# Transposing softmax probabilities on TensorE as two 16-bit halves of each word

## The chip, the cores and the metric

The kernel runs on one core of a Trainium2 chip. A core has a matrix engine (TensorE, PE in the profile; its weight loads are listed apart as PEld), a vector engine (VectorE, DVE), a scalar engine (ScalarE, ACT), GpSimd (POOL) and a queue for transfers (SyncE, SP). TensorE reads SBUF and writes PSUM; a matmul holds one operand in the array (it is loaded by a weight load) and streams the other through it. The metric is the time of one execution on the device in microseconds.

## The reference

The reference is a gated cross-attention block followed by a gated, quantized feed-forward block, on `x` of shape (2, 2048, 512) and a context of 77 tokens for each of the 2 batches.

```python
q = (layernorm(x) @ Wq.T + bq)            # 16 heads of 32
k, v = ctx @ Wk.T + bk, ctx @ Wv.T + bv   # 77 keys
attn = softmax(q @ k.T / sqrt(32))        # per head, 2048 x 77
x = x + tanh(g_xattn) * ((attn @ v) @ Wo.T + bo)
h = gelu(qlinear(layernorm(x), w1, b1))   # 512 -> 2048, 8-bit grid, per-tensor scale
x = x + tanh(g_ffn) * qlinear(h, w2, b2)  # 2048 -> 512
```

Everything is float32. `qlinear` rounds its input and its weight to 255 levels by the largest magnitude of the whole tensor.

## The kernel before

The 4096 rows are worked in 8 blocks of 512 rows (`NB = 8`, `TB = 512`), each as 4 row tiles of 128 (`NT = 4`). The kernel has three stages: attention for all blocks (up to about 423 us of the profiled execution, with the end of the last block's output projection and the scale of the quantization up to about 449 us), the first feed-forward product with GELU, and the second product with the output.

The change lies in the attention stage. The 16 heads are worked as 4 groups of 4 heads (`NG = 4`, `HG = 4`), and a block has 8 steps `s`: a step is one head group and one half (2 of the 4 row tiles). The functions of a step, with their lines:

- `project_q` (L257): 4 accumulating fp32 matmuls (8 instructions) make `pq`; ScalarE adds the bias into `qT`.
- `softmax` (L270): TensorE makes the scores of 2 row tiles and 4 heads in PSUM (`ps`, L279, 8 instructions); VectorE takes the maximum (L288) and subtracts it (L292); ScalarE exponentiates in place (L298); VectorE sums (L300) and inverts (L302); GpSimd multiplies (L303). The result `e`, 128 rows by 2 x 4 x 77 float32 probabilities, lies in one of 3 SBUF buffers.
- `transpose_a` (L309), called twice for each step (`u` = 0 and 1): TensorE transposes the four 128 x 77 pieces of one row tile into one PSUM tile `pta` (L316), where the probabilities are the loaded operand (77 columns) and the identity the streamed one (128 columns), and ScalarE copies the PSUM tile into `aT` (L317), 77 keys by 4 heads by 512 rows.
- `apply_v` (L319): when a head group's `aT` is complete, 4 fp32 matmuls (8 instructions, `pc`) multiply by the values; ScalarE copies to `cT` (L333).
- `project_o` (L335): the output projection of one row tile of the block before (`po`, 8 instructions); VectorE adds it to `x`.
- `transpose_x` (L241): normalizes a row tile of the next block, transposes it in fp32 (`ptx`, L251, 128 columns loaded), and ScalarE copies to `xnT` (L252).

The PSUM pool `ps_t` has two buffers, shared by `pta` and `ptx`: a third transposed tile cannot be written before the first one has been copied out. `ps_s` (scores) and `ps_p` (projections and `pc`) have two each.

The loop goes over the blocks and their 8 steps. In each step it issues the softmax of two steps ahead, then the first `transpose_a`, then by the step's number an `apply_v` and a `project_o` (even steps), a `project_q` or two `transpose_x` (odd steps), and the second `transpose_a`. This program order is the priority with which a planner lists the instructions of each engine; it works with estimated costs, and may put later work ahead where an instruction is not ready by its estimate. Each engine then runs its list in order. Only the start of the kernel and the feed-forward stage have an order written out by hand. Around the step, `weight_step` puts the quantization of the feed-forward weights on VectorE, and `load_x` puts the loads of later blocks on SP's queue; a `project_q` of the next block needs all four of its `xnT` copies.

`ident` is a 128 x 128 float32 identity and `identb` the same in bf16 (L123); the latter is used before the change for the transposes of quantized rows alone (`px`, L180).

Of the kernel before, what the change touches and what calls it, by code (L numbers as in the profile page):

```python
# [7 lines left out]

F32 = mybir.dt.float32
BF16 = mybir.dt.bfloat16  # L10
AF = mybir.ActivationFunctionType
ALU = mybir.AluOpType
AX = mybir.AxisListType
# [2 lines left out]
P = 128  # L16
D = 512
KC = D // P
HEADS = 16
DK = D // HEADS  # L20
NK = 77
HG = P // DK
# [20 lines left out]
def tile_flamingo_gated_block(  # L43
# [20 lines left out]
    nc = tc.nc  # L64
# [56 lines left out]
    ident = const.tile([P, P], F32, name="ident")  # L121
    make_identity(nc, ident)
    identb = const.tile([P, P], BF16, name="identb")  # L123
    nc.vector.tensor_copy(identb, ident)
# [4 lines left out]

    w1q = const.tile([P, KC, FF], BF16, name="w1q")  # L130
    xqT0 = const.tile([P, KC, TB], BF16, name="xqT0")
    w2q = const.tile([P, FC, D], BF16, name="w2q")
    mean2 = const.tile([P, NB, NT, 2], F32, name="mean2")
# [16 lines left out]
    def scale_of(maxima, name, psum, tag):  # L150


        m = const.tile([P, 1], F32, name=f"m_{name}")
        nc.vector.tensor_reduce(m, maxima, AX.X, ALU.max)
        diag = small.tile([P, P], F32, tag="diag", name=f"diag_{name}", bufs=1)
        nc.vector.tensor_scalar(diag, ident, m, None, ALU.mult)
        pg = psum.tile([P, 512], F32, tag=tag, name=f"pg_{name}")
        nc.tensor.matmul(pg[:, :P], ones, diag, start=True, stop=True)
        g = const.tile([P, 1], F32, name=f"g_{name}")
        nc.vector.tensor_reduce(g, pg[:, :P], AX.X, ALU.max)  # L160
        s = const.tile([P, 1], F32, name=f"s_{name}")
        nc.vector.tensor_scalar(s, g, MIN_RANGE, 1.0 / QP, ALU.max, ALU.mult)
        inv = const.tile([P, 1], F32, name=f"inv_{name}")
        nc.vector.reciprocal(inv, s)
        return s, inv
# [12 lines left out]
    def transpose_q(dst, src):  # L178
        for kc in range(KC):
            nc.tensor.transpose(dst[:, kc, :], src[:, kc * P : (kc + 1) * P], identb)  # L180
# [10 lines left out]
    with actx:  # L191
        ps_s = actx.enter_context(tc.tile_pool(name="ps_s", bufs=2, space=PSUM))
        ps_t = actx.enter_context(tc.tile_pool(name="ps_t", bufs=2, space=PSUM))
# [5 lines left out]
        def project_k(b, g):  # L199
# [10 lines left out]
            for j in range(HG):  # L210
# [3 lines left out]
                if j % 2:  # L214
                    nc.scalar.activation(dst, pk[r, :NK], AF.Identity, bias=bias)
                else:
# [15 lines left out]
        ln, xnT, qT, aT, cT, es = {}, {}, {}, {}, {}, {}  # L232
# [24 lines left out]
        def project_q(i, g):  # L257
# [9 lines left out]
            qT[i, g] = work.tile([P, TB], F32, tag="qT", name=f"qT{i}_{g}", bufs=5)  # L267
            nc.scalar.activation(qT[i, g], pq, AF.Identity, bias=bq_sb[:, g : g + 1])

        def softmax(i, s):  # L270
# [26 lines left out]
            ).ins  # L297
            last["ACT"] = nc.scalar.activation(e, e, AF.Exp, scale=SCALE).ins  # L298
            sm = small.tile([P, 2, HG], F32, tag="sm", name=f"sm{n}")
# [9 lines left out]
        def transpose_a(i, s, u):  # L309
            g, half = divmod(s, 2)  # L310
            t = 2 * half + u
            if t == 0:
                aT[i, g] = work.tile([NK, HG, TB], F32, tag="aT", name=f"aT{i}_{g}", bufs=3)
            pt = ps_t.tile([P, KC, P], F32, tag="pt", name=f"pta{i}_{s}_{u}")
            for j in range(HG):
                nc.tensor.transpose(pt[:NK, j, :], es[i, s][:, u, j, :], ident)  # L316
            nc.scalar.copy(aT[i, g][:, :, t * P : (t + 1) * P], pt[:NK, :, :])  # L317

        def apply_v(i, g):  # L319
            pc = ps_p.tile([P, TB], F32, tag="pp", name=f"pc{i}_{g}")  # L320
# [116 lines left out]
        for i in range(NB):  # L437
            for s in range(2 * NG):
                if s + 2 < 2 * NG:
                    last = softmax(i, s + 2)  # L440
                elif i + 1 < NB:
                    last = softmax(i + 1, s + 2 - 2 * NG)
                transpose_a(i, s, 0)

                if i == 0 and s < 2:
# [3 lines left out]
                if i == 0 and s == 2:  # L449


                    with tc.issue_after(last["ACT"]):
                        nc.scalar.activation(tg, tg, AF.Tanh)
                    with tc.issue_after(last["POOL"]):
# [10 lines left out]
                if i + 1 < NB:  # L465
# [3 lines left out]
                    if s in (3, 5):  # L469
                        for t in (s - 3, s - 2):  # L470
                            transpose_x(i + 1, t)
                transpose_a(i, s, 1)
                if s in (5, 7) and i + 1 < NB:
                    project_q(i + 1, (s - 5) // 2)
# [15 lines left out]
                t = s - NT if i == 0 else s // 2  # L490
# [11 lines left out]
        warm = small.tile([P, 1], F32, tag="warm", name="warm")  # L502
        nc.scalar.activation(warm, cT[NB - 1, NG - 1][:, 0:1], AF.Gelu)
        for t in range(NT):
# [7 lines left out]
        s_x, inv_x = scale_of(xmax, "x", ps_p, "pp")  # L512
        xq0 = work.tile([P, NT, D], BF16, tag="xnT", name="xq0", bufs=1)
        for t in range(NT):
# [4 lines left out]
            else:  # L519
                nc.scalar.activation(v, v, AF.Copy, bias=MAGIC, scale=inv_x)  # L520
                last = nc.vector.tensor_scalar(vq, v, MAGIC, None, ALU.subtract).ins
        for t in range(NT):
            px = ps_t.tile([P, KC, P], BF16, tag="pt", name=f"px0_{t}")
            transpose_q(px, xq0[:, t, :])
# [21 lines left out]
    with ExitStack() as fctx:  # L546
# [22 lines left out]
        for i in range(NB):  # L569
# [4 lines left out]
            for a in range(GT):  # L574
                G = gtile(f"G{i}_{a}")
                for v in range(GF // 2):
# [18 lines left out]
                    k = (i * GT + a) * 2 + v  # L595
                    n = 1 if k == NB * GT * 2 - 1 else 2
# [129 lines left out]
```

## Time and profile before

| | |
|---|---|
| median of 3 runs | 692.16 us (690.68 to 694.86) |
| profiled execution | 692.1 us, span 690.0 us from the first to the last instruction |
| mean granted TensorE clock | 0.985 |
| TensorE busy | 651.0 us (94%) |
| VectorE busy | 518.4 us (75%) |
| ScalarE busy | 342.9 us (50%) |
| GpSimd busy | 200.7 us (29%) |
| transposes of the probabilities, L316 | 512, 280 ns from start to end each |
| copies out of PSUM, L317 | 128, 579 ns each |

A row of groups names the line, the engine, the operation, the tile written and the tiles read, the shapes and the count; behind the bar stand the busy time and the mean length of one, behind the second bar the idle time of the engine just before, with what ended it. In the timeline the first column is the start, the second the length of a run of like instructions, merged. In the table of stretches the columns are the length, the busy times with the number of instructions (in the order PE, PEld, DVE, ACT, POOL, where an engine has any), the granted clock, the share of the transfer engines, and GB/s. The chain that ended last lists what the end waited for, step by step; "issue" is time in which nothing seen in the profile was waited for.

### The profile page before, as it was taken

How to read it: one execution, taken by the hardware profiler on the slowest of the kernel's cores; microseconds unless marked ns; L12 is line 12 of the kernel's file. 1: busy time of each engine (PE TensorE's matmuls, PEld its weight loads, DVE VectorE, ACT ScalarE, POOL GpSimd, SP SyncE). 2: the span in 40 equal slices, each digit the busy share in tenths (PEclk: the TensorE clock that was granted, in tenths of full speed). 3: DMA queues.
4: the chain of work that ended last, by engine and by line, in shares of the span. 5: the costliest groups of instructions: out<-in, count | busy, mean ns of one | idle time of the engine just before them, and what ended most of it. 6: DMA issues, size and time to landing. Idle time of an engine off the chain costs nothing.

```text
span 690.0 us, 8178 instructions
## 1 busy us (share of the span) xinstructions
PE 651.0 (94%) x3027; PEld 324.3 (47%) x3048; DVE 518.4 (75%) x799; ACT 342.9 (50%) x472; POOL 200.7 (29%) x160
## 2 busy tenths in 40 slices
PE   4999999999999999999999999599999979999987
PEld 2655555455555455555455454244444424444433
DVE  3674686996996996975965757899998779865452
ACT  2455443344443344444344333179898979344540
POOL 2234323233233233233333332100000029991000
PEclk9999999999999999999999999799999989999999
DMA  9901100031131131100000000059999608798872
GB/s 299 353 2 58 65 1 0 1 119 65 62 123 61 62 117 66 62 0 1 1 0 1 1 16 1 0 153 353 318 312 358 183 9 345 262 347 321 315 275 76
DMA packets 41663, 89.09 MB, mean 129 GB/s; under 512 B 18763, under 2 KB 18763, under 8 KB 35480
## 3 DMA queue, kind: packets, MB, share of 16 engines
q1 hardware_dynamic: 39752, 87.21, 36.2%
q10 hardware_dynamic: 1872, 1.37, 0.7%
q8 instruction: 24, 0.39, 0.2%
q14 instruction: 15, 0.12, 0.1%
HBM read 51.34 MB, written 33.55 MB: 123 GB/s over the span
## 4 chain that ended last, share of the span: by engine, by line
PE 77%; DMA 8%; DVE 8%; ACT 4%; issue 2%; POOL 0%; SPq 0%; ACTq 0%; DVEq 0%
PE ph L581 16%; PE po L338 16%; PE pq L260 15%; PE pta L316 8%; DMA Gb<-h 7%; PE ps L279 6%; PE pf L643 6%; PE pc L325 6%; PE ptx L251 2%; ACT Gb L634 2%; DMA x<-in_x 1%; PE pvv L223 1%; PE pk L203 1%; DVE xf L169 1%; DVE tm L360 1%
## 5 line engine op out<-in xcount | busy, mean ns | idle before, releaser
L303 POOL TENSOR_TENSOR e<-e,rs 128x616 f32<-128x616 f32 x64 | 78.4, 1226 | 255.3 <-DVE rs L302 192.4
L643 PE MATMUL pf<-w2q,hq 128*128 128x512 bf16 x502 | 114.9, 388 | 8.4 <-DVE hq L635 4.6
L260 PE MATMUL pq<-xnT,wq_sb 128*128 128x512 f32 x256 | 117.9, 604 | 2.0 <-ACT xnT L252 2.0
L338 PE MATMUL po<-wo_sb,cT 128*128 128x512 f32 x256 | 117.6, 604 | 0.0
L581 PE MATMUL ph<-xqT,w1q 128*128 128x512 bf16 x501 | 111.3, 382 | 1.3 <-DVE xqT L526 0.5
L317 ACT COPY aT<-pta 77x512 f32<-77x512 f32 x128 | 72.4, 579 | 77.8 <-PE pta L316 77.7
L588 ACT ACTIVATE G<-ph,b1s,s 128x512 f32<-128x512 f32 x128 | 99.5, 777 | 14.0 <-PE ph L581 3.1
L657 POOL TENSOR_TENSOR x<-x,b_sb 128x512 f32<-128x512 f32 x32 | 57.8, 1848 | 125.2 <-DVE b_sb L614 125.2
L643 PEld LDWEIGHTS <-hq 128*128 128x128 bf16 x512 | 50.6, 100 | 72.4 <-issue 8.3
L598 DVE TENSOR_REDUCE hmax<-G 128x1 f32<-128x1024 f32 (+1 forms) x65 | 76.5, 1197 | 10.4 <-ACT G L588 10.3
L316 PE MATMUL pta<-ident,e 128*77 128x128 f32 x512 | 79.3, 280 | 1.7 <-ACT aT L317 1.2
L338 PEld LDWEIGHTS po<-wo_sb,cT 128*128 128x128 f32 x256 | 46.2, 189 | 71.7 <-issue 70.4
L581 PEld LDWEIGHTS <-w1q 128*128 128x128 bf16 x512 | 50.3, 99 | 62.0 <-issue 2.1
L316 PEld LDWEIGHTS pta<-ident,e 128*77 128x77 f32 x512 | 59.8, 147 | 40.6 <-issue 34.3
L298 ACT ACTIVATE e<-e 128x616 f32<-128x616 f32 x64 | 45.9, 717 | 60.2 <-DVE e L292 56.1
L288 DVE TENSOR_REDUCE mx<-ps 128x8 f32<-128x616 f32 x64 | 49.9, 780 | 30.3 <-PE ps L279 30.1
L260 PEld LDWEIGHTS pq<-xnT,wq_sb 128*128 128x128 f32 x256 | 46.8, 193 | 51.2 <-issue 47.2
L634 ACT ACTIVATE Gb<-Gb,inv_h 128x2048 f32<-128x2048 f32 x24 | 47.6, 1999 | 45.9 <-DMA Gb<-h 43.9
L300 DVE TENSOR_REDUCE sm<-e 128x8 f32<-128x616 f32 x64 | 50.4, 789 | 24.2 <-ACT e L298 23.9
L635 DVE TENSOR_SCALAR hq<-Gb 128x2048 bf16<-128x2048 f32 x24 | 38.2, 1600 | 30.5 <-ACT Gb L634 30.5
L292 DVE TENSOR_TENSOR e<-ps,mx 128x616 f32<-128x616 f32 x64 | 50.9, 796 | 2.9
L279 PE MATMUL ps<-kb,qT 64*128 64x154 f32 x512 | 52.7, 319 | 0.2
(89 smaller groups left out, 594.4 us busy)
## 6 DMA issues: line engine op xcount, KB each, us to landing
h<-G SPq DMA_DIRECT2D x24, 1024.0 KB, 6.2
Gb<-h SPq DMA_DIRECT2D x24, 1024.0 KB, 8.2
raw_w<-in_w2T SPq DMA_DIRECT2D x8, 1024.0 KB, 5.0
out_y<-x SPq DMA_DIRECT2D x32, 256.0 KB, 4.4
x<-in_x SPq DMA_DIRECT2D x7, 1024.0 KB, 5.4
raw_w<-in_w1T SPq DMA_DIRECT2D x4, 1024.0 KB, 11.7
x<-in_x SPq DMA_DIRECT2D x4, 256.0 KB, 3.5
wq_sb<-in_wqT ACTq DMA_DIRECT2D x1, 1024.0 KB, 9.6
```

The lines of the kernel that those rows point to most:

```text
L260: nc.tensor.matmul(pq, wq_sb[:, kc, g * P : (g + 1) * P], xnT[i][:, kc, :], start=(kc == 0), stop=(kc == KC - 1),)
L279: nc.tensor.matmul(ps[:, q, u * RK : (u + 1) * RK], qT[i, g][r, t * P : (t + 1) * P], kblk[i // NBB][r, g, :], start=True, stop=True,)
L303: last["POOL"] = nc.gpsimd.tensor_tensor(e4, e4, rs[:, :, :, None].to_broadcast([P, 2, HG, NK]), ALU.mult).ins
L316: nc.tensor.transpose(pt[:NK, j, :], es[i, s][:, u, j, :], ident)
L317: nc.scalar.copy(aT[i, g][:, :, t * P : (t + 1) * P], pt[:NK, :, :])
L338: nc.tensor.matmul(po, cT[i, g][:, t * P : (t + 1) * P], wo_sb[:, g, :], start=(g == 0), stop=(g == NG - 1),)
L581: nc.tensor.matmul(ph, w1q[:, kc, fc * P : (fc + 1) * P], cur[:, kc, :], start=(kc == 0), stop=(kc == KC - 1),)
L588: nc.scalar.activation(G[:, 2 * v + u, :], ph, AF.Gelu, bias=b1s[:, fc : fc + 1], scale=s1,)
L598: nc.vector.tensor_reduce(hmax[:, k + u : k + u + 1], G[:, 2 * v + u : 2 * v + u + n, :], AX.XY, ALU.max, apply_absolute_value=True,)
L634: nc.scalar.activation(rest, rest, AF.Copy, bias=MAGIC, scale=inv_h)
L643: nc.tensor.matmul(po[t], hq[:, fc, t * P : (t + 1) * P], w2q[:, fc, :], start=(fc == 0), stop=(fc == FC - 1),)
L657: nc.gpsimd.tensor_tensor(y, y, b2_sb, ALU.add)
```

## The change

A float32 word is seen as two 16-bit halves. For each head, TensorE transposes the low halves and the high halves apart, as bf16 with the bf16 identity, so that the PSUM tile has 4 heads x 2 halves x 128 rows of 16 bits: the same 2 KB a partition as before. A transpose moves the bits as they are. ScalarE's copy reads the PSUM tile as unsigned 16-bit integers in its order, and writes each half to its place in the words of `aT`, that is with a distance of two 16-bit elements. The number of copies stays, each with twice the elements; the number of transposes doubles. The loaded operand of a transpose is 77 elements of 2 bytes that lie 4 bytes apart.

```diff
+U16 = mybir.dt.uint16
...
-            pt = ps_t.tile([P, KC, P], F32, tag="pt", name=f"pta{i}_{s}_{u}")
+
+            pt = ps_t.tile([P, HG, 2, P], BF16, tag="pt", name=f"pta{i}_{s}_{u}")
             for j in range(HG):
-                nc.tensor.transpose(pt[:NK, j, :], es[i, s][:, u, j, :], ident)
-            nc.scalar.copy(aT[i, g][:, :, t * P : (t + 1) * P], pt[:NK, :, :])
+                halves = es[i, s][:, u, j, :].bitcast(BF16).rearrange("p (k h) -> p k h", h=2)
+                for h in range(2):
+                    nc.tensor.transpose(pt[:NK, j, h, :], halves[:, :, h], identb)
+            dst = aT[i, g][:, :, t * P : (t + 1) * P].bitcast(U16)
+            nc.scalar.copy(dst.rearrange("p j (n h) -> p j h n", h=2), pt[:NK].bitcast(U16))
```

## The prediction

> **What bounds the kernel now.** I read the page first, from the top: engines, slices, and the chain that ended last.
>
> ```profile
> PE 651.0 (94%) x3027; PEld 324.3 (47%) x3048; DVE 518.4 (75%) x799; ACT 342.9 (50%) x472; POOL 200.7 (29%) x160
> ...
> PE   4999999999999999999999999599999979999987
> ...
> ACT  2455443344443344444344333179898979344540
> ...
> PE 77%; DMA 8%; DVE 8%; ACT 4%; issue 2%; POOL 0%; SPq 0%; ACTq 0%; DVEq 0%
> ```
>
> The change lies in the attention stage, roughly slices 2 to 24 (30 to 423 us). TensorE (PE) is at 9 there in every slice and ScalarE (ACT) at 3 to 5. Next I asked for the stretch from 60 to 423 us, all engines and then the transposes' tile `pta` alone (PE, weight loads, ACT).
>
> ```profile
> 60.00:423.00 363.00, 358.03 (x1717) 184.93 (x1715) 280.19 (x491) 151.04 (x257) 121.24 (x100) 1.00 0.12 42
> ...
> 60.00:423.00 363.00, 71.80 (x464) 54.44 (x464) 65.63 (x116) 1.00 0.12 42
> ```
>
> PE is busy 358.0 of 363 us at a granted clock of 1.00; ACT 151.0 of 363, so it has room in sum. A nanosecond more on PE here is a nanosecond more on the end, while one on ACT counts only where PE waits for it. Then the groups of the two lines that change.
>
> ```profile
> L316 PE MATMUL pta<-ident,e 128*77 128x128 f32 x512 | 79.3, 280 | 1.7 <-ACT aT L317 1.2 <-POOL e L303 0.5
> L317 ACT COPY aT<-pta 77x512 f32<-77x512 f32 x128 | 72.4, 579 | 77.8 <-PE pta L316 77.7
> L316 PEld LDWEIGHTS pta<-ident,e 128*77 128x77 f32 x512 | 59.8, 147 | 40.6 <-issue 34.3 <-PE po L338 1.7 <-ACT aT L317 1.6
> ```
>
> The 280 ns are an instruction's length from start to end, not its price; instructions overlap, and the price is the step from one start to the next. The timeline gives steps: of n merged pieces, (stretch − one's length) / (n − 1). In the rows below the second column is the stretch.
>
> ```profile
> 274.03 0.60 PE L316 MATMUL pta<-ident,e 128*77 128x128 f32 x4
> 303.25 1.04 PE L251 MATMUL ptx<-ident,xn 128*128 128x128 f32 x8
> 20.26 0.86 PEld L203 LDWEIGHTS pk<-ctx_sb,wk_sb 128*128 128x128 f32 x7
> 460.01 2.04 PEld L581 LDWEIGHTS <-w1q 128*128 128x128 bf16 x10
> 446.03 1.04 PE L180 MATMUL px<-identb,xq 128*128 128x128 bf16 x8 [0.46 <-DVE xq L185]
> 444.90:447.60 2.70, 2.09 (x16) 1.54 (x16) 0.50 0.00 0
> ```
>
> Row by row: (0.60 − 0.273)/3 = 109 ns a step for today's fp32 transpose. (1.04 − 0.273)/7 = 110 ns for the one with 128 stationary columns: the same, so today the 128 streamed columns set the step, not the load. (0.86 − 0.19)/6 = 112 ns for the K projection, which streams only 77 columns: there the load of 128 fp32 columns sets it, 0.87 ns a column. (2.04 − 0.10)/9 = 216 ns for 512 bf16 columns, 54 ns for 128. Last, the only bf16 transposes of this kernel: (1.04 − 0.31)/7 = 104 ns, but at a granted clock of 0.50 (the last row, third number from its end).
>
> **What it removes and adds on PE.** 128 tiles of 4 fp32 transposes, 512 × 109 ns = 55.8 us (the chain agrees: `pta` is 7.8% of 690.0, 53.8 us), become 128 tiles of 8 bf16 transposes, 1024 in all. Their stream is 128 bf16 columns, 54 ns. Their load is 77 columns of 2-byte elements that lie 4 bytes apart, for which no row exists. Lower bound: loads stay under the stream, as in the `w1q` row: 1024 × 54 = 55.3 us, −0.5 us. Upper bound: every bf16 transpose steps as the `px` rows did, 104 ns: 106.5 us, +50.7 us; that row ran at half clock and is far from this stage. Between: the load costs what an fp32 column costs in the `pk` row, 77 × 0.87 = 67 ns, is longer than the 54 ns stream and so sets the step: 1024 × 67 = 68.6 us, **+12.8 us**. I take this one: same partitions, same 77 columns and the same 4-byte distance between columns as the fp32 load that it replaces. Nothing covers it, since PE is at 9 in every slice.
>
> Two rules of the Trainium skill speak against the change. TensorE: Matmul & The Clock Gate, section "Weight-path perf modes", says that the fast weight load needs all 128 columns; 77 would not get it, and by that page's load rule the step would be about 64 ns, an estimate near the one above. No row here shows a 77-column bf16 load. The same page, section "Back-to-back issue gap", puts a sustained load-and-matmul pair with 128 streamed columns at about 81 ns; by it the sum on PE would be 1024 × 81 − 55.8 = +27 us, an estimate, and no run here shows it.
>
> **What it adds on ACT.** The copy reads 1024 16-bit elements for 512 words. Does ACT pay by element or by byte?
>
> ```profile
> L526 ACT COPY xqT<-px 128x512 bf16<-128x512 bf16 x2 | 1.2, 586 | 1.2 <-PE px L180 1.2
> ...
> L634 ACT ACTIVATE G<-G,inv_h 128x2048 f32<-128x2048 f32 x7 | 13.3, 1987 | 0.0
> ...
> L634 ACT ACTIVATE G<-G,inv_h 128x1536 f32<-128x1536 f32 x1 | 1.6, 1577 | 2.6 <-DVE s L612 2.6
> ```
>
> By element: 512 bf16 take 586 ns, like 512 fp32 (579). Another 512 cost (1987 − 1577) = 410 ns. So 0.58 becomes 0.99 us, +0.41. Bounds: +0 (pairs written as words) and +0.58 (two copies of 512); I take 0.41, as 1024 elements lie between the two shapes of L634's row. In sum 128 × 0.41 = 52.5 us more on ACT, hidden by its idle time: in a block of some 52 us ACT goes from about 21 to 28 us. It shows where PE waits for a copy, as `ps_t` has two buffers and a third transpose tile waits for the first one's copy. The chain shows one such place a block; it is the fifth of a block's eight steps, where two x transposes sit between two probability transposes.
>
> ```profile
> 312.82 0.59 ACT aT L317
> ...
> 313.45 0.67 PE ptx L251 x4
> ...
> 314.14 0.59 ACT xnT L252
> ...
> 314.78 3.70 PE pq L260 x8
> ```
>
> The aT copy releases `ptx`, whose copy releases the next Q projection: the copy's +0.41 passes on to PE once a block, in the 7 blocks that prepare a next one: 7 × 0.41 = 2.9 us. The end of the stage is the other place; the transposes of the last two steps find nothing between them.
>
> ```profile
> 420.85 0.66 PE L316 MATMUL pta<-ident,e 128*77 128x128 f32 x4 [0.23 <-ACT aT L317]
> ...
> 422.18 1.07 PE L325 MATMUL pc<-aT,vb 77*32 77x512 f32 x8 [0.67 <-ACT aT L317]
> ```
>
> Three copies in a row there: 3 × 0.41 = 1.2 us. Sum of waits **+4.1 us** (bounds 0 and 10 × 0.58 = 5.8). Elsewhere: in most blocks `apply_v` (pc) comes 1.3 us of PE work after the transposes whose copy it needs (0.72 for ps, 0.59 for the next tile), and a copy of 0.99 plus 0.08 of hand-over fits under that, by 0.2 us. If the cover goes, each of 32 pc waits up to 0.41: +13 us. Behind the longer copies in ACT's queue stand the exponentials; they come up to 0.8 us later, but a softmax is issued two steps (about 13 us) before its transposes and needs some 5 us (0.78 + 0.80 + 0.72 + 0.79 + 0.20 + 1.23 plus hand-overs), so PE doesn't see it. DVE and POOL wait for those exponentials and have idle time. No DMA is issued or moved, and the SP and POOL queues are as before. The order of PE's instructions comes from a planner, which will place things a little otherwise with longer copies; I cost that at nothing, since the softmaxes give it work to fill with, and it is inside the range.
>
> **The sum.** The profiled execution took 692.1 us (span 690.0 plus 2.1 around it), the median of the runs is 692.16: no difference. 692.1 + 12.8 + 4.1 = **709 us**.
>
> **Rivals.**
> A. The strided load is as quick as the packed one: PE −0.5, waits +4.1: 695.7 us. For it: the `w1q` loads take 0.10 us each at full length against 0.147 for `pta`. Against: those have 128 packed columns.
> B. Loads and streams don't overlap as well, or ScalarE's copies become late for pc as well: a step of 77 ns, a quarter of the way from 67 to the 104 of the `px` rows, adds 1024 × 10 ns = 10 us to 709, or the 32 pc waits add 13: 719 to 722 us. For it: the spare time ahead of pc is only 0.2 us, and with qT's 0.69 us ahead in ACT's queue it is less. Against: PE's own growth of 0.1 us a tile widens that cover.
> C. The other side, not slower: the load is quick, and the tile's first load, which nothing covers when it follows a ps group (4 transposes take 0.59 there against 0.44 after a projection), is halved. With 0.07 us less on about 64 of the 128 tiles that is −4.5 us, against the waits' +4.1: 692.1 − 0.5 − 4.5 + 4.1 = 691 us, and 687 if the planner also hides the waits. It decides if a bf16 pair steps at 54 ns or less.
> D. The change doesn't do what it says: no; twice the instructions must run, they can't be merged.
>
> **How the numbers follow.** Main case 0.47 (its own range 703 to 715: load 64 to 70 ns, waits 0 to 5.8), A 0.22, B 0.21, C 0.10. The range that leaves out under 2 in 10 goes from A to B: 695 to 722; the 747 of the half-clock row (692.1 + 50.7 + 4.1) is left out, as that clock is absent here. Half a per cent, 3.5 us, is about what a measurement of this kernel can tell from no change (the three runs span 4.2). Faster by more than that: 0.03, from C with hidden waits. Within it: 0.10, the rest of C and a little of A. Slower: 0.87.
>
> **What would show it.** In the profile after: 1024 transposes at L320 or so, their step 67 ns (8 in about 0.54 + 0.2 us); 54 would be A, 77 or more B. The aT copy at 0.99 us. PE's idle time ahead of `ptx`, pq and pc `<-ACT aT` growing from about 4 us to 8. The attention stage ends at about 440 instead of 423 us, everything behind it shifted by as much and unchanged. The prediction is wrong if the strided load is priced otherwise than by columns, if the 16-bit strided write slows ACT past 1.2 us, or if the planner reorders PE so that it waits in new places.

## The result, and the profile after

The changed kernel takes 711.99 us (median of 4 runs, 711.38 to 714.47) against 691.42 us: 1.0286 times the kernel before, with a 95% interval of 1.0257 to 1.0315, or 20.6 us more. The prediction was 709 us in a range of 695 to 722. The time is where it was expected; neither of the two terms that were added up for it is, as the profile shows at once. From the page after (engines, then the groups of the two changed lines, busy time and mean length behind the first bar):

```profile
PE 659.7 (93%) x3539; PEld 333.5 (47%) x3560; DVE 520.0 (73%) x799; ACT 429.8 (61%) x472; POOL 201.2 (28%) x160
...
PE 66%; ACT 11%; DMA 8%; DVE 7%; POOL 5%; issue 2%; SPq 1%; ACTq 0%; DVEq 0%
...
L322 ACT COPY aT<-pta 77x1024 uint16<-77x1024 uint16 x128 | 164.0, 1304 | 58.7 <-PE pta L320 58.2
...
L320 PEld LDWEIGHTS <-e 128*77 128x77 bf16 x1024 | 67.8, 117 | 43.3 <-issue 41.5
...
L320 PE MATMUL pta<-identb,e 128*77 128x128 bf16 x1024 | 80.3, 221 | 3.3 <-ACT aT L322 1.8
```

On the chain that ended last, TensorE (PE) fell from 77% to 66% and ScalarE (ACT) rose from 4% to 11%. Some five points of TensorE's fall went to GpSimd (POOL, 0% to 5%), since the chain takes another branch in the output stage at the very end; only ScalarE's rise belongs to the change. The copy takes 1.304 us, where 0.99 was predicted. And the timeline gives the step of the new transposes:

```profile
310.93 0.61 PE L320 MATMUL pta<-identb,e 128*77 128x128 bf16 x8
```

(0.61 − 0.22)/7 = 56 ns, where 67 was predicted. So the 16-bit transposes cost nearly nothing more than the fp32 ones, and the copies cost what they should not have. Where it shows in a block, in the chain after, in step s = 5 of a block (counted from 0, so the sixth of the eight; the prediction called it the fifth):

```profile
324.36 0.46 PE pta L320 x8
324.82 0.02 issue
324.84 2.59 ACT aT L322 x2
327.43 0.44 ACT xnT L253
327.87 0.62 ACT e L299
328.49 0.48 ACT xnT L253
328.97 0.04 issue
329.01 3.70 PE pq L261 x8
```

This is the place that the prediction named. Before, one copy of 0.59 us stood there (312.82) and TensorE's own `ptx` was a link of the chain. Now two copies, both x copies and an exponential stand in a row on ScalarE, and TensorE waits for the last of them.

Everything after the attention stage is unchanged. The first matmul of the feed-forward stage (its start is the first of the two starts in these rows, before and then after) moved by 19.9 us, of 20.2 us in the spans:

```profile
L581 PE MATMUL ph<-xqT,w1q x501: 379/379/634, 448.3 to 559.9; 128*128 128x512 bf16 x167
```

```profile
L586 PE MATMUL ph<-xqT,w1q x501: 379/379/634, 468.2 to 580.1; 128*128 128x512 bf16 x167
```

That start is the measure used below beside the times: it leaves out the later stages, which differ by up to 3.6 us from run to run. The theory on record was that the strided load sets the step, +12.8 us, and that the copies add 4.1 us. The theory formed from this profile: the load is hidden, and nearly all the loss is ScalarE's copy, longer than predicted and late in more places.

### The profile page after: what moved, and what is told of

Its sections match the earlier page's. It is cut to its first block, busy times and chain, and to the rows that moved or that the text cites. A ratio compares the mean times of both kernels' runs of the same rounds, so it can differ in the third digit from the quotient of the medians.

```text
span 710.2 us, 9137 instructions
## 1 busy us (share of the span) xinstructions
PE 659.7 (93%) x3539; PEld 333.5 (47%) x3560; DVE 520.0 (73%) x799; ACT 429.8 (61%) x472; POOL 201.2 (28%) x160
## 4 chain that ended last, share of the span: by engine, by line
PE 66%; ACT 11%; DMA 8%; DVE 7%; POOL 5%; issue 2%; SPq 1%; ACTq 0%; DVEq 0%
PE ph L586 15%; PE po L343 15%; PE pq L261 15%; DMA Gb<-h 7%; ACT aT L322 6%; PE pc L330 6%; PE pta L320 5%; POOL x L662 4%; PE ps L280 4%; PE pf L648 2%; ACT Gb L639 2%; PE ptx L252 1%; ACT e L299 1%; DMA x<-in_x 1%; ACT xnT L253 1%
## 5 line engine op out<-in xcount | busy, mean ns | idle before, releaser
L322 ACT COPY aT<-pta 77x1024 uint16<-77x1024 uint16 x128 | 164.0, 1304 | 58.7 <-PE pta L320 58.2
L261 PE MATMUL pq<-xnT,wq_sb 128*128 128x512 f32 x256 | 120.3, 614 | 3.5 <-ACT xnT L253 3.2
L320 PEld LDWEIGHTS <-e 128*77 128x77 bf16 x1024 | 67.8, 117 | 43.3 <-issue 41.5
L603 DVE TENSOR_REDUCE hmax<-G 128x1 f32<-128x1024 f32 (+1 forms) x65 | 77.6, 1223 | 10.6 <-ACT G L593 10.5
L320 PE MATMUL pta<-identb,e 128*77 128x128 bf16 x1024 | 80.3, 221 | 3.3 <-ACT aT L322 1.8
L280 PE MATMUL ps<-kb,qT 64*128 64x154 f32 x512 | 55.8, 320 | 1.0
L269 ACT ACTIVATE qT<-pq,bq_sb 128x512 f32<-128x512 f32 x32 | 22.0, 688 | 51.8 <-PE pq L261 51.8
```

The lines of the kernel that those rows point to most:

```text
L261: nc.tensor.matmul(pq, wq_sb[:, kc, g * P : (g + 1) * P], xnT[i][:, kc, :], start=(kc == 0), stop=(kc == KC - 1),)
L280: nc.tensor.matmul(ps[:, q, u * RK : (u + 1) * RK], qT[i, g][r, t * P : (t + 1) * P], kblk[i // NBB][r, g, :], start=True, stop=True,)
L320: nc.tensor.transpose(pt[:NK, j, h, :], halves[:, :, h], identb)
L322: nc.scalar.copy(dst.rearrange("p j (n h) -> p j h n", h=2), pt[:NK].bitcast(U16))
L603: nc.vector.tensor_reduce(hmax[:, k + u : k + u + 1], G[:, 2 * v + u : 2 * v + u + n, :], AX.XY, ALU.max, apply_absolute_value=True,)
```

## The experiments

### The two costs by themselves

Nothing of the computation is done (`x` goes to the output); 48 transposes of each load form run in one stream, and then 6 copies of each form.

```diff
+        for k in range(48):   # 77 columns, 2 bytes each, 4 bytes apart
+            nc.tensor.transpose(th[:NK, k % HG, k // HG % 2, :], half[:, k % HG, :, 1], identb)
...
+        for k in range(R):    # packed on both sides
+            nc.scalar.copy(d16, tw16)
+        for k in range(R):    # as in the change: the write has a distance of two elements
+            nc.scalar.copy(inter, th16)
+        for k in range(R):    # the read has a distance of 128 elements, the write is packed
+            nc.scalar.copy(
+                d16.rearrange("p j (n h) -> p j n h", h=2), th16.rearrange("p j h n -> p j n h")
+            )
```

> The two disputed costs by themselves. This kernel leaves out the whole computation (x is copied to the output) and runs 48 transposes of each load form in one stream, then 6 copies of each form. Theory on record (the strided 16-bit load sets the step): bf16 transposes with 77 columns that lie 4 bytes apart step at about 67 ns, and those with 77 packed columns at 54 to 56 ns. Rival, from the trace of the changed kernel: both step at 56 ns, fp32 at 109 ns. Copies on ScalarE: priced by element, 1024 16-bit elements take 0.99 us in every layout, contiguous or strided; priced by layout, the contiguous ones take 0.99 us, and only the write with a distance of two elements takes 1.30 us; if it is the distance on either side, a strided read with a packed write takes 1.30 us as well; if it is the 16-bit integer type, the same copy as bf16 is back at 0.99 us.

The groups of this run (L96: fp32, 77 columns; L98: bf16, 128 packed columns; L100: bf16, 77 packed; L102: bf16, 77 with the distance; L111 to L125: copies on ACT; L113 is packed on both sides, L115 and L123 have the distance in the write, L117 in the read):

```profile
L123 ACT COPY dst<-th 77x1024 bf16<-77x1024 bf16 x6 | 7.7, 1287 | 0.2
L115 ACT COPY dst<-th 77x1024 uint16<-77x1024 uint16 x6 | 7.7, 1287 | 0.2
...
L113 ACT COPY dst<-tw 77x1024 uint16<-77x1024 uint16 x6 | 6.0, 1008 | 0.2
...
L117 ACT COPY dst<-th 77x1024 uint16<-77x1024 uint16 x6 | 6.0, 1007 | 0.2
...
L96 PE MATMUL tw<-ident,xb 128*77 128x128 f32 x48 | 5.4, 273 | 0.0
...
L111 ACT COPY dst<-tw 77x512 f32<-77x512 f32 x6 | 3.5, 581 | 42.6 <-PE tw L96 42.4
L100 PE MATMUL th<-identb,eb 128*77 128x128 bf16 x48 | 2.8, 220 | 0.0
L98 PE MATMUL th<-identb,xh 128*128 128x128 bf16 x48 | 2.8, 219 | 0.0
L102 PE MATMUL th<-identb,xb 128*77 128x128 bf16 x48 | 2.8, 220 | 0.0
L98 PEld LDWEIGHTS <-xh 128*128 128x128 bf16 x48 | 2.8, 98 | 0.0
...
L102 PEld LDWEIGHTS <-xb 128*77 128x77 bf16 x48 | 2.7, 117 | 0.0
```

All three bf16 forms take 2.8 us for 48, (2.8 − 0.22)/47 = 55 ns a step; fp32 takes (5.4 − 0.27)/47 = 109. The 77-column load is longer from start to end (117 against 98 ns), and hidden all the same. The load term of the prediction falls. Two halves cost 2 × 56 = 112 ns against 109 for the word: splitting a word saves nothing, as both stream 128 columns and the word streams at half the rate.

A copy of 1024 16-bit elements takes 1.008 us packed, and the predicted 0.99 was right for that. The write with a distance of two 16-bit elements costs 0.28 us more; a read with a distance of 128 elements costs nothing (1.007); the type does not matter (bf16 1.287). That the price lies in the write was not among the bounds of the prediction (at most 1.16 us).

### TensorE's part alone

Against the changed kernel; both transposes take the high half, so the numbers that go on are wrong.

```diff
-                    nc.tensor.transpose(pt[:NK, j, h, :], halves[:, :, h], identb)
-            dst = aT[i, g][:, :, t * P : (t + 1) * P].bitcast(U16)
-            nc.scalar.copy(dst.rearrange("p j (n h) -> p j h n", h=2), pt[:NK].bitcast(U16))
+                    nc.tensor.transpose(pt[:NK, j, h, :], halves[:, :, 1], identb)
+            words = pt[:NK].rearrange("p j h n -> p j (h n)").bitcast(F32)
+            nc.scalar.copy(aT[i, g][:, :, t * P : (t + 1) * P], words)
```

> TensorE's part of the change alone: eight 16-bit transposes for each tile, but the copy is that of 512 words as before (0.58 us). Both transposes take the high half, so the numbers that go on are not the probabilities. Theory on record: the load steps at 67 ns, 692 + 12.8 = 705 us. Rival (TensorE steps at 56 ns; the loss lies with ScalarE's copy): 1024 x 56 - 512 x 109 = +1.5 us, 693 us.

695.53 us, 1.0045 times (1.0023 to 1.0066), +3.1 us with an interval of 1.6 to 4.6 (3.8 us by the medians). The stage ended 2.0 us later:

```profile
L586 PE MATMUL ph<-xqT,w1q x512: 378/380/635, 450.3 to 562.6; 128*128 128x512 bf16 x171
```

That is 1024 × 56 − 512 × 109 = +1.5 us and a little more. The 12.8 us are refuted.

### ScalarE's part alone, in two doses

The four fp32 transposes stay, and only the copy is changed. Both are shown against the kernel before. Strong dose, a distance of two elements on both sides:

```diff
-            nc.scalar.copy(aT[i, g][:, :, t * P : (t + 1) * P], pt[:NK, :, :])
+            dst = aT[i, g][:, :, t * P : (t + 1) * P].bitcast(U16)
+            nc.scalar.copy(
+                dst.rearrange("p j (n h) -> p j h n", h=2),
+                pt[:NK].bitcast(U16).rearrange("p j (n h) -> p j h n", h=2),
+            )
```

> ScalarE's part alone: four fp32 transposes for each tile as before, and a copy of 1024 16-bit elements, low halves first and then high halves of each head, with a distance of two elements on both sides. Theory on record (copy 0.99 us, about ten places where it is late): 692 + 4 = 696 us. Rival (the copy takes 1.30 us or more and is late in every block): 692 + 18 = 710 us.

Middle dose, packed on both sides:

```diff
+            dst = aT[i, g][:, :, t * P : (t + 1) * P].bitcast(U16)
+            nc.scalar.copy(dst, pt[:NK].bitcast(U16))
```

> The middle dose: four fp32 transposes for each tile as before, and a copy of 1024 16-bit elements in their order, contiguous on both sides. If a 16-bit element costs the same in every layout, this copy is as long as that of the changed kernel, 1.30 us, and the time is that of the other copy experiment, 710 us by the rival. If the distance in the write makes the difference, it takes 0.99 us and the time lies between: 692 + 18 x (0.99 - 0.58)/(1.30 - 0.58) = 702 us if lateness grows in proportion, 696 us if waits are paid only at the ten places of the prediction.

Strong dose (copy 1.302 us): 715.10 us, 1.0332 times (1.0291 to 1.0373), +23 us, more than the whole change. Middle dose (1.005 us): 702.28 us, 1.0148 times (1.0100 to 1.0196), +10.5 us. The copies, and the start of the feed-forward stage, of the strong and then of the middle dose:

```profile
L319 ACT COPY aT<-pta 77x1024 uint16<-77x1024 uint16 x128 | 163.3, 1302 | 57.5 <-PE pta L317 57.2
L586 PE MATMUL ph<-xqT,w1q x512: 378/380/635, 470.9 to 583.4; 128*128 128x512 bf16 x171
```

```profile
L319 ACT COPY aT<-pta 77x1024 uint16<-77x1024 uint16 x128 | 126.9, 1005 | 63.5 <-PE pta L317 63.2
L583 PE MATMUL ph<-xqT,w1q x512: 378/380/635, 458.0 to 570.0; 128*128 128x512 bf16 x171
```

The stage ended 22.6 us and 9.7 us later. In the strong dose some 3 of the 22.6 us are not lateness but the clock: from 442 to 448 us it was granted at 0.50, and the last pc and po took 1.94 + 16.14 us where the middle dose has 1.07 + 13.95. The copy reads with a distance of two here and is as long as with the distance in the write alone (1.302 against 1.304 us), so this read costs nothing either. With TensorE's transposes as before, the copy alone makes the loss, and its dose sets it. The middle dose is the copy that the prediction had in mind; for it the prediction had 4.1 us. The chain of the middle dose shows what was missed:

```profile
312.30 0.46 PE ps L280 x2
312.76 0.99 PE pc L327 x8
313.75 3.63 PE po L340 x8
317.38 0.44 PE pta L317 x4
317.82 0.72 PE ps L280 x6
318.54 0.61 PE pta L317 x4
319.14 0.02 issue
319.17 1.01 ACT aT L319
320.17 0.48 ACT xnT L253
320.66 0.62 ACT e L299
321.27 0.48 ACT xnT L253
321.75 0.04 issue
321.80 1.55 PE pq L261 x3
```

Two changes of the planner's order. It puts 2 of the 8 scores of a later softmax ahead of pc, as it may where an instruction is late by its estimate; those take 0.46 us, and the other six take 0.72, as long as all eight did before (311.46 in the chain before). And it lists the exponential `e` between the two x copies, where before it came behind them. Both were costed at nothing in the prediction. Two runs below take them back, the exponential first.

### The distance on the read side

The changed kernel with the copy turned round.

```diff
-            nc.scalar.copy(dst.rearrange("p j (n h) -> p j h n", h=2), pt[:NK].bitcast(U16))
+            nc.scalar.copy(
+                dst.rearrange("p j (n h) -> p j n h", h=2),
+                pt[:NK].bitcast(U16).rearrange("p j h n -> p j n h"),
+            )
```

> The changed kernel with one thing turned round: the copy reads the halves with a distance (n after h in the reading order) and writes words in order, the same values to the same places. Theory now (the distance in the 16-bit write costs 0.28 us of each copy, and the loss is the lateness of ScalarE's copies): the copy takes 1.01 us and the time is that of the middle dose plus the small part of TensorE, 702 to 705 us. Rival (the loss does not follow the copy's length): 712 us as in the changed kernel.

707.39 us (704.17 to 709.03), 1.0210 times (1.0172 to 1.0248). The copy takes 1.005 us as expected, and the time is 4.6 us under that of the changed kernel; the two ratios' intervals do not meet, so the distance in the write is shown to be a cause. The time is still 2 us over what was expected. The profiled execution shows a reason that was not thought of: the granted clock from 420 to 450 us (the third number from the end) is 0.94, where the middle dose has no such dip. A mean of 0.94 over 30 us is 1.8 us lost. The stage ended at 461.8 us, 6.4 us earlier than in the changed kernel, and 8.2 without the dip.

```profile
L589 PE MATMUL ph<-xqT,w1q x512: 379/379/634, 461.8 to 573.8; 128*128 128x512 bf16 x171
```

```profile
420.00:450.00 30.00, 27.18 (x125) 13.09 (x124) 20.41 (x43) 9.82 (x12) 7.92 (x8) 0.94 0.00 1
```

### The exponential behind the x copies

On top of the strided read; the softmax of step 5 is cut before its exponential, and the rest is issued after the second `transpose_x`.

```diff
-                    last = softmax(i, s + 2)
+                    late = s == 5 and i + 1 < NB
+                    last = softmax(i, s + 2, late)
...
-                            transpose_x(i + 1, t)
+                            copied = transpose_x(i + 1, t)
+                        if s == 5:
+                            with tc.issue_after(copied):
+                                last = finish(i, s + 2)
```

> As the run with the strided read, and in step 5 of each block the exponential of the softmax ahead is put behind the second copy of the next block's x on ScalarE (in the trace it stands between the two, 0.62 us on the chain, in the 7 blocks that prepare a next one). If that place is on the path: 7 x 0.6 = 4 us less than the strided read, 698 to 700 us. If the exponential had the time anyhow, or its softmax is late afterwards: no difference.

702.98 us, 1.0151 times (1.0123 to 1.0179), 4.4 us less than the strided read. That difference fits the expectation, but the trace does not support the reason.

```profile
L598 PE MATMUL ph<-xqT,w1q x512: 379/379/634, 459.2 to 571.5; 128*128 128x512 bf16 x171
```

The stage ended at 459.2 us against 461.8, and 1.8 of those 2.6 us are the dip of the clock that this execution did not have; another 2.1 us of the two profiled executions' difference lie in the later stages, which were not changed. From the chain, a block gained 0.24 us (its part from `pta` to pq took 4.17 us instead of 4.41), since with the exponential gone the chain goes through `ptx` again, as before the change, with 1.01 us for the copy in place of 0.59. The first block gave 0.5 us back (its successor's first Q projection starts at 57.84 us against 57.33), so the exponential's place was worth about 1 us in all, not 4.

### No filler ahead of pc

On top of that, the scores of the same softmax are told to come behind pc.

```diff
+            after = tc.issue_after(pc_last[i]) if late else ExitStack()
+            with after:
```

> As the run with the late exponential, and the planner's filler is taken out: with the longer copy it puts the first 2 of the 8 score instructions of the seventh softmax ahead of apply_v (pc) of the second head group, in 6 blocks; here those scores are told to come behind that pc. By the chain the two take 0.46 us ahead of pc and the other six as long as all eight did (0.72), so the split costs 0.46 us a block while pc would be ready within 0.1 us: 6 x 0.4 = 2.4 us less, the first feed-forward product starts at 456.8 instead of 459.2 us, 700 us in all. What is then left against the kernel before, 8 us, should be the 2 us of TensorE's part, and the places that the prediction counted (10 x 0.41 = 4.1 us), with 2 us over. Rival: pc waits as long as the filler took, no difference.

702.57 us, 1.0116 times (1.0062 to 1.0171): by the median no difference to the run before it. Each against the kernel before as measured together with it, the two are 8.8 and 10.6 us slower, 1.8 us apart, but the intervals of the ratios overlap. The last block's pc started at 430.77 us, against 433.16 in the run with the filler, 2.4 us earlier as expected; but then the profiled execution lost it again. Chain lines of that end without the filler:

```profile
427.89 2.84 ACT aT L329 x3
430.77 1.79 PE pc L340 x8
432.56 16.57 PE po L354 x32
```

and with it:

```profile
430.28 2.84 ACT aT L327 x3
433.16 1.07 PE pc L338 x8
434.23 13.95 PE po L351 x32
```

The same matmuls, 1.79 + 16.57 against 1.07 + 13.95 us: 3.3 us more. In the table of stretches the granted clock of the run without the filler (third number from the end) is low there:

```profile
428.00:434.00 6.00, 4.14 (x24) 1.64 (x22) 4.77 (x11) 4.10 (x5) 1.01 (x1) 0.75 0.01 3
434.00:440.00 6.00, 6.00 (x11) 2.38 (x10) 2.03 (x5) 0.69 (x2) 0.00 (x0) 0.68 0.00 0
440.00:446.00 6.00, 6.00 (x16) 2.65 (x15) 4.03 (x11) 0.00 (x0) 1.35 (x2) 1.00 0.00 0
```

Less those 3.3 us, the feed-forward stage would have begun at 460.2 − 3.3 = 456.9 us, against the expected 456.8 (the same 2.4 us seen at the end, not a second measurement). That the filler is worth 2.4 us is shown up to pc by the trace; by the time it is not, since the clock covers it.

### Only the high half, and rounded probabilities

If a 16-bit transpose has half the price of a word, the low half is what the change pays for. Leaving out the low 16 bits:

```diff
+            pt = ps_t.tile([P, HG, P], BF16, tag="pt", name=f"pta{i}_{s}_{u}")
...
+                nc.tensor.transpose(pt[:NK, j, :], halves[:, :, 1], identb)
+            nc.scalar.copy(aT[i, g][:, :, t * P : (t + 1) * P], pt[:NK])
```

> Leaves out the low 16 bits of the probabilities: four bf16 transposes of the high halves for each tile, and a copy of 512 bf16 elements to fp32 (0.58 us). If a 16-bit transpose is 56 ns wherever it stands and TensorE bounds this stage: 692 - 512 x (109 - 56) = 692 - 27 = 665 us. If another engine takes over as the bound (VectorE has 282 us of work in a stage that would last some 340): 670 to 680 us. By the theory on record (67 ns): 670 us.

672.99 us, 0.9707 times (0.9673 to 0.9741), 19.4 us less than before; the stage ended 19.2 us earlier. The time lies in the 670 to 680 us that were expected if another engine takes over, and not at 665. By the sum, TensorE's work fell by 27 us (512 transposes at 56 ns in place of 109), so 8 us were lost again. Most of them are waits of TensorE: the Q projections wait 3.6 us for copies of x (2.0 before), the scores 2.1 us for `qT` (at most 0.2 before), and the transposes 3.3 us for GpSimd's products, where before it was 0.5:

```profile
L319 PE MATMUL pta<-identb,e 128*77 128x128 bf16 x512 | 48.5, 222 | 4.0 <-POOL e L304 3.3 <-ACT aT L320 0.4
```

The same with packed, rounded values:

```diff
+            eb = work.tile([P, 2, HG, NK], BF16, tag="eb", name=f"eb{n}", bufs=3)
...
-                e4, e4, rs[:, :, :, None].to_broadcast([P, 2, HG, NK]), ALU.mult
+                eb, e4, rs[:, :, :, None].to_broadcast([P, 2, HG, NK]), ALU.mult
```

> The probabilities are rounded to bf16 by GpSimd's multiplication, which writes them to a tile of their own, so the low 16 bits are left out here too, with rounding in place of cutting off; the 77 columns of a transpose's load are then packed, 2 bytes apart. If packing matters to the load, it is faster than the run of high halves by up to 512 x 11 ns = 6 us; if loads are hidden in both, the same time, 665 us.

674.24 us, 0.9738 times (0.9706 to 0.9770): no difference to the high halves. Packing a load gave nothing here, where the stream hides it. Both are faster than either kernel, at the price of 16 bits of every probability.

## Why the prediction was right or wrong

**What bounds the kernel: right.** TensorE's order and ScalarE's lateness in the attention stage decide, and nothing behind the stage changed.

**The load of 77 strided columns, +12.8 us: wrong.** The step that failed is "I take this one", the choice of the K projection's 0.87 ns a column, measured on fp32 columns, for 16-bit ones. The step is 56 ns, 2 ns above the lower bound of that part, and the term is +2.0 us at the end of the stage (+3.1 us by the time, 1.6 to 4.6). The two rules of the Trainium skill's TensorE: Matmul & The Clock Gate that were weighed there did not hold here either: a step of 64 ns, an estimate by the load rule of "LDWEIGHTS (loading the stationary operand)", and about 81 ns for a sustained pair by "Back-to-back issue gap", stand against 55 to 56 ns in two kernels.

**The copy's length, 0.99 us: wrong, because of its write.** By element it is 1.005 us, as worked out; the distance in the 16-bit write adds 0.28 to 0.30 us, and no row of before has such a write. The text had it among what would make the prediction wrong ("if the 16-bit strided write slows ACT past 1.2 us").

**The waits, +4.1 us: right place, much too small.** With TensorE's 2.0 us taken off, the copies cost 19.9 − 2.0 = 17.9 us. The split is not exact: the strong dose alone cost 22.6 − 3 = some 19.5 us, so that beside late copies TensorE's part adds less than by itself.

For a copy of the predicted length the middle dose gives 458.0 − 448.3 = 9.7 us. A block far from the ends is 1.13 us longer than before (from the Q projection that step 5 holds up to the next such one, 269.63 to 321.80 us against 263.74 to 314.78). Of these, the 0.42 us of the longer copy in step 5 were predicted, as 0.41. Missing were 0.24 us for the exponential's place and 0.46 us for the planner's filler; taken back, they gave about 1 us and 2.4 us in all. Seven such blocks make 7.9 us. The end of the stage adds 1.6 us, where 1.2 was predicted: five copies on ScalarE are on the chain there and not three. "I cost that at nothing", said of the planner's order, is the step that failed.

What is left to 17.9, 8.2 us, goes with the last 0.3 us of the copy; it is what the strided read takes back. A block of the changed kernel is 0.64 us longer than one with that read (276.01 to 329.01 us against 271.09 to 323.45): 0.24 us in step 5, 0.24 ahead of transposes near the block's end, where TensorE now waits for a copy (1.32 us at 286.96), and 0.07 ahead of the pc of the first head group (a copy of 1.21 us at 305.14). In the first block it is 2 us, one of them a half clock (below), and at the end of the stage about 2 us, with six late copies.

**The sum.** −10.8 us on the load and +13.8 us on the waits offset each other; the 709 us were close by luck. The rivals were nearer in kind: A for the load, and the second half of B, late copies, for the rest, though B put them ahead of pc, and most fell elsewhere. C's saving did not come: behind scores, a tile's transposes take 0.57 us in the chain after and 0.59 before.

## What to carry to other kernels

A longer instruction on an engine with idle time isn't hidden by that idle time: where its result hands back one of two PSUM buffers, 0.42 us more on 128 copies (54 us) gave 10 us on the end, and 0.72 us gave 18 to 20. When ScalarE copies 16-bit elements from PSUM to SBUF, put a distance between them on the reading side, not on the writing side. A word split into two 16-bit halves gains nothing on TensorE, since a word's transpose (109 ns a step) costs what two halves do (2 × 56); only a half left out does.

## What the runs showed of the hardware that was not expected

- ScalarE: 1024 16-bit elements from PSUM to SBUF in 1.008 us, with a distance of two elements in the write 1.287, with one of 128 elements in the read 1.007. The page SBUF — State Buffer, section "Door 1: The DMA port swizzle", counts hits in lines of 16 bytes and would let a step of 4 bytes pass free, without naming reads or writes; for this write the measurement differs.
- VectorE's copy of the same packed 1024 took 0.686 us, as long as that of 512 fp32 words, and 1.286 with the distance in the write; with the distance of 128 in the read it took 1.220, so that on VectorE the reading side is hardly better.
- Waits at the end of the stage were followed by a granted clock of 0.5 for some us in some executions and not in others. The run without the filler had 0.50 from 431 to 437 us after copies of 2.84 us, and lost 3.3 us; the one with it, after the same 2.84 us, kept 1.00. The strong dose of copies had 0.50 from 442 to 448 us after 3.60 us, and the changed kernel kept 1.00 there after 3.77 and 3.62 us. In the changed kernel it happened in the first block, where the clock was 0.50 from 59 to 61 us and a Q projection of 3.70 us took 4.66. The page TensorE: Matmul & The Clock Gate, Part 1, has a free-running window of some 3.4 us for this, which would make it a matter of chance. The waits here are about as long as that window or shorter, with some work of TensorE in them, and no run was made to test it. So a wait added on TensorE can cost more than its length.
- A stream of fp32 transposes alone came to a steady 109 ns a step, but not at once. In the run of forms the first 64 fp32 transposes after an idle start were busy for 8.6 us, (8.6 − 0.3)/63 = 132 ns a step, and the next 48 for 5.4 us, 109 ns a step; the start is slower by 1.4 us in all, though the granted clock stands at 1.00 from 25 to 30 us, over that start.
